# Copying gathered rows through ScalarE and gathering into half-chunk buffers in a two-layer relational graph network

## The chip, the core and the metric

The kernel runs on one core of a Trainium2 chip. The metric is device time in microseconds (us), from the start of the program on that core to its end. Five engines work in parallel, each through its own instructions in order: TensorE (PE in the profile; PEld is its weight load, which overlaps the matmuls), VectorE (DVE), ScalarE (ACT), GpSimd (POOL) and SyncE (SP). They are kept in step by semaphores: an instruction can wait until others have raised a semaphore, and raises one itself when it is done. POOL issues the gathers, SP the regular transfers.

## The reference

The kernel computes a relational graph network of two layers over 50,000 nodes with 128 features, followed by a residual layer norm. There are 16 relations whose matrices are mixtures of 8 bases, and 800,000 random edges and 50,000 self loops, sorted by their target.

```python
def _rgcn_layer(h, src, dst, rel, basis, w_comp, loop_w, bias):
    W = jnp.einsum('rb,bio->rio', w_comp, basis)
    seg = dst.astype(jnp.int32) * N_REL + rel.astype(jnp.int32)
    agg = jax.ops.segment_sum(h[src], seg, num_segments=N_ENT * N_REL)
    agg = agg.reshape(N_ENT, N_REL, -1)
    msg = jnp.einsum('nri,rio->no', agg, W)
    out = msg + h @ loop_w + bias
    return jax.nn.relu(out)
h = layer(layer(x))                       # two layers with their own weights
return _layernorm(x + h, axis=-1)
```

## The kernel before

The kernel does not sum by relation. For each of the 8 bases it sums, for every node, the rows of its neighbours weighted by the basis's share in the edge's relation, and then multiplies the 8 sums by the 8 basis matrices. The self loops are treated apart ("own", line 794), so that 800,000 edges are gathered in each of the two layers.

The unit of work is a tile of 128 edges. Ten tiles (K) make a chunk, and a layer has 625 chunks (C), so both layers together have 12,500 tiles. The edges are in the order of their targets. A chunk's first and last five tiles form two halves. For each chunk:

- POOL issues ten gathers (`gather`, line 260): each is an indirect DMA that fetches 128 rows of 512 bytes by a list of indices into one [128, 128] slice of a buffer `rows[...]`. There are four such buffers of ten tiles (GATHERS = 4). At chunk c, the ten gathers of chunk c+2 are issued (FETCH = 2, lines 1090 to 1093), into the buffer that chunk c-2 used. The first of them goes to the slice that PE reads last, so it carries the wait for PE's last matmul of chunk c-2. Each gather also waits until the gather eight earlier has landed, since there are eight semaphores ("lanes") for them.
- DVE builds the weighted one-hot matrices of a chunk (`hot_of`, lines 988 and 995: 128x2400 numbers, three buffers), two chunks ahead.
- PE multiplies, tile by tile, the gathered rows (as the loaded weights) by the tile's one-hot matrix (128x240): line 1112. The products of each half accumulate in a PSUM bank `pa` (six banks in layer 1, four in layer 2). In the trace each such matmul has two records.
- DVE adds the products to the running sums `ring` (`add`, line 1016, four adds of 128x240 for a chunk). They are queued eight tiles after the chunk's last matmul (ADDED = 8).

Around this runs the work of groups of 512 nodes, 98 in each layer: ScalarE lays out the group's own features (line 787) and DVE multiplies them into the ring (line 794) with a table that SP loads (line 776, 1 MB each); once a group's edges are all added, ScalarE copies its 128x4096 sums out of the ring (`copy`, line 814); PE multiplies them by the bases (line 818) on top of the loop weights (line 828); ScalarE applies relu (line 833); PE turns the result back (line 845), and it is stored (lines 853 to 863; in layer 2 with the layer norm, lines 611 to 622). ScalarE also widens the gather indices once for 16 chunks (`indexed`, line 951; a cast at line 953) and, in layer 1, moves the weights of the edges (line 694).

The order on PE, POOL, DVE and ScalarE is written out by hand (line 982). The loop over chunks emits the gathers and matmuls; everything else is put into a heap of events by `later(time, ...)` with times counted in tiles (ten for a chunk), and `go_on` emits what is due after each tile. So each engine's queue holds the events between the tiles at fixed places, in order.

Of the kernel before, what the change touches and what calls it, by code (L numbers as in the profile page):

```python
# [40 lines left out]
F32 = mybir.dt.float32  # L41
# [10 lines left out]
P = 128  # L52
# [4 lines left out]
K = 10  # L57
# [6 lines left out]
FETCH = 2  # L64
AT = 8
PER = 5
# [1 line left out]
BANK = 512  # L68
WEIGHTS = AT * PER * 8
BITS_AT_ONCE = 168  # L70
GATHERS = 4
J = 4
AHEAD = 16
EACH = 2 * len(WINDOWS)
# [20 lines left out]
def tile_rgcn_resnorm(  # L95
# [15 lines left out]
    nc = tc.nc  # L111
    N, D = x.shape
# [3 lines left out]
    C = -(-M // (K * P))  # L116
# [31 lines left out]
    consts = ctx.enter_context(tc.tile_pool(name="consts", bufs=1))  # L148
# [110 lines left out]
    def gather(to, of, idx):  # L259
        return nc.gpsimd.indirect_dma_start(  # L260
            out=to, out_offset=None, in_=of, in_offset=bass.IndirectOffsetOnAxis(ap=idx, axis=0)
        )
# [11 lines left out]
        return bass.AP(tensor=edges.tensor, offset=edges.offset + j * E + first, ap=ap)  # L274


    rows = [consts.tile([P, K, D], F32, name=f"g{i}") for i in range(GATHERS)]
    src = consts.tile([P, 2 * C * HALF], U16, name="src")
    key = consts.tile([P, 2 * C * HALF], U8, name="key")

# [312 lines left out]
    def count_up(pool):  # L593
        pick = pool.tile([P, 2], F32, name="pick")
        nc.vector.tensor_reduce(pick[:, 0:1], squares, AX.X, OP.add)
        nc.vector.tensor_reduce(pick[:, 1:2], picked, AX.X, OP.add)
        total = banks.take()
        nc.tensor.matmul(total[:1, :2], ones[:, 0:1], pick, start=True, stop=True)
        off = pool.tile([1, 2], F32, name="off2")
        nc.vector.tensor_scalar(off[:, 0:1], total[:1, 0:1], float(N), None, op0=OP.not_equal)  # L600
        nc.vector.tensor_scalar(
            off[:, 1:2], total[:1, 1:2], float(E + 2 * NG * (P + 1) + 2 * C), None, op0=OP.not_equal
        )
        nc.vector.tensor_tensor(bad, off[:, 0:1], off[:, 1:2], op=OP.max)
# [19 lines left out]
    def chunked():  # L624
        with (
# [5 lines left out]
            def ks(c):  # L631
                return min(K, -(-M // P) - c * K)
# [7 lines left out]
            def behind_of(c):  # L640
                return ADDED if c < C - 2 else PER
# [285 lines left out]
            def done(steps):  # L927
                for _ in steps:
                    pass
# [18 lines left out]
            index = {}  # L948

            def indexed(n, b, copy):  # L950
                first_of, end_of = b * AHEAD * K, min(C, (b + 1) * AHEAD) * K
                index[n, b] = hp.tile([P, AHEAD * K], I32, name="index", bufs=3)
                return copy(index[n, b][:, : end_of - first_of], src[:, first_of:end_of])
# [28 lines left out]
            ordered.enter_context(tc.manual_schedule(engines={mybir.EngineType.PE, mybir.EngineType.Pool, mybir.EngineType.DVE, mybir.EngineType.Activation}))  # L982
            for n, of in enumerate((x, H1)):

                def hot_of(c):
                    pm = batches[c // BATCH].pm
                    own = fixed[:, WN : WN + K * WN].rearrange("e (k w) -> e k w", w=WN)
                    nc.vector.tensor_tensor(  # L988
                        own,
                        grid[:, None, :].to_broadcast([P, K, WN]),  # L990
                        key[:, c * K : (c + 1) * K, None].to_broadcast([P, K, WN]),
                        op=OP.is_equal,
                    )
                    hot = hp.tile([P, K, NB, WN], F32, name="hot", bufs=3)
                    nc.vector.tensor_tensor(  # L995
                        hot,
                        pm[:, c % BATCH * K * NB : (c % BATCH + 1) * K * NB].rearrange("e (k b) -> e k b", b=NB)[:, :, :, None].to_broadcast([P, K, NB, WN]),
                        own[:, :, None, :].to_broadcast([P, K, NB, WN]),
                        op=OP.mult,
                    )  # L1000
                    hots[c] = hot
# [23 lines left out]
                def added_up_to(now):  # L1025
                    while behind and behind[0][0] <= now:
                        for one in sorted(behind.pop(0)[1], key=lambda one: (-one[1], one[2])):
                            add(*one)
# [20 lines left out]
                def go_on(now):  # L1049
                    while events and events[0][0] <= now:  # L1050
                        _, _, what, args = heapq.heappop(events)
                        what(*args)
# [10 lines left out]
                for c in range(C):  # L1063
                    if c >= 2:
                        later(K * (c - 2) + ADDED, hot_of, c)
# [14 lines left out]
                for c in range(C):  # L1080
                    if (c + FETCH + 3) % AHEAD == 0 and c + FETCH + 3 < C:
                        indexed(n, (c + FETCH + 3) // AHEAD, nc.scalar.copy)
                    if n == 0 and c == C - AHEAD // 2:
                        indexed(1, 0, nc.scalar.copy)
                    if n == 0 and c:

                        next(coming, None)
                        while ready[0] + 1 < len(ROWS) and 2 * min(C, c + FETCH + AHEAD + 4) > ROWS[ready[0] + 1]:
                            next(coming)
                    for to in range(0 if c == 0 else c + FETCH, min(C, c + FETCH + 1)):  # L1090
                        buffer = (n * C + to) % GATHERS
                        for k in (PER, *range(PER), *range(PER + 1, K)) if to + 1 < C else range(K):
                            gather(rows[buffer][:, k, :], of, index[n, to // AHEAD][:, to % AHEAD * K + k : to % AHEAD * K + k + 1])
                    g = rows[(n * C + c) % GATHERS]
                    if c == 0:
                        hot_of(0)
                        hot_of(1)
                    hot = hots.pop(c)
                    mine_of = []
                    for half in range(2):  # L1100
                        pa = banks.take(Once(added, c), OWN[n])
                        tiles = [(i, j) for i, (j0, j1) in enumerate(PARTS_OF) for j in range(j0, j1)]
                        tiles = [(i, j) for i, j in tiles if half * PER + j < ks(c)]
                        if c + 1 < C:
                            tiles.reverse()
                        mine = [[t for t in tiles if t[0] == i] for i in range(len(PARTS_OF))]
                        for at in range(PER):
                            if at < len(tiles):
                                i, j = tiles[at]
                                j0, j1 = PARTS_OF[i]  # L1110
                                w, before = WINDOWS[i], NB * sum(WINDOWS[:i])
                                nc.tensor.matmul(  # L1112
                                    pa[:, before : before + NB * w],
                                    g[:, half * PER + j, :],
                                    hot[:, half * PER + j].rearrange("e b w -> e (b w)"),
                                    start=(i, j) == mine[i][0],
                                    stop=(i, j) == mine[i][-1],
                                )
                            now = c * K + half * PER + at
                            if at == PER - 1:  # L1120
                                mine_of.extend((c, half, i, pa) for i in range(len(PARTS_OF)) if mine[i])
                                if half:
                                    behind.append((now + behind_of(c), mine_of))
                            added_up_to(now)
                            if n == 0 and c == 0:
                                for _ in range(2 if now < K - 1 else P):
                                    if next(first_runs, started) is started:
                                        started.clear()
                                        break
                            if c or now == K - 1:  # L1130
                                go_on(now)
                    if n == 0 and c == 3:
                        beginning.close()
                    if n == 0 and c == C - 1:
                        done(coming)
                        count_up(pr)
# [9 lines left out]
    def summed():  # L1146
        L1 = dram.tile([N, D], F32, name="L1")
        L2 = dram.tile([N, D], F32, name="L2")
        with tc.tile_pool(name="io", bufs=2) as io, tc.tile_pool(name="sbf", bufs=2) as sb:
# [152 lines left out]
            nodes(L2, norm, also=x)  # L1302

    chunked()
    wrong = nc.values_load(bad[0:1, 0:1], min_val=0, max_val=1)
    with tc.If(wrong > 0):
# [40 lines left out]
```

## Time and profile before

| | |
|---|---|
| time, median of 3 runs | 18022.98 us (18019.99 to 18026.41) |
| profiled execution | 17926.77 us, span 17925.0 us |
| mean granted TensorE clock | 0.718 |
| PE busy, matmuls | 9549.2 us (53%) |
| DVE busy | 7645.9 us (43%) |
| ACT busy | 1608.6 us (9%) |
| POOL busy | 11865.7 us (66%) |
| gathers | 12500, of which 6250 in each layer |
| bytes moved | 1525.45 MB, mean 85 GB/s |

The busy times are of one execution. No engine is busy more than two thirds of the time, so the time is set by how the engines wait for each other. Such waits are read from the groups of instructions, where each group has its busy time, the mean duration of one instruction in ns, and then the idle time of its engine just before the instructions with what ended it; and from the list of waits, which has the total in us, how often, and the longest. "issue" there is idle time in which the profile shows nothing that the engine waited for, and "remote" a wait that ended by a signal that the profile could not put down to an instruction.

### The profile page before, as it was taken

What the parts mean: (1) busy time and instruction counts of PE and PEld (TensorE: products, weight loads), DVE (VectorE), ACT (ScalarE), POOL (GpSimd) and SP (SyncE); (2) the same over time, 40 slices, a digit from 0 to 9 for tenths busy, and PEclk for the clock granted to TensorE, in tenths of its full rate; (3) what the DMA queues carried; (4) which work ended last, traced back from release to release, by engine and by line L of the source; (5) the groups of instructions that cost most, each with busy time, mean ns of one, the idle gap of its engine ahead of it and who ended that gap; (6) DMA issues with size and microseconds to landing.
All of it is one profiled execution on the core that took longest, in us unless ns stands there. A gap on an engine that the chain in (4) does not pass through costs nothing.

```text
span 17925.0 us, 102973 instructions
## 1 busy us (share of the span) xinstructions
PE 9549.2 (53%) x31567; PEld 6859.0 (38%) x31567; DVE 7645.9 (43%) x11001; ACT 1608.6 (9%) x2031; POOL 11865.7 (66%) x12540
## 2 busy tenths in 40 slices
PE   4555555555555555555545555555555555555555
PEld 3443334333333434343333333333333333333333
DVE  5554445454333433343334443444444344444433
ACT  1011101001000100000000000000000000000000
POOL 6666666666666666666666666666666666666666
PEclk7777777777777777777777777767777777777777
DMA  3333333333222222222222222222222222222222
GB/s 106 93 96 96 95 95 92 92 92 89 85 85 85 87 85 85 83 85 86 81 80 82 82 81 81 82 81 82 80 80 79 82 82 82 82 82 82 82 80 70
DMA packets 790743, 1525.45 MB, mean 85 GB/s; under 512 B 227861, under 2 KB 294279, under 8 KB 790182
## 3 DMA queue, kind: packets, MB, share of 16 engines
q0 software_dynamic: 401872, 826.89, 16.4%
q1 hardware_dynamic: 386566, 691.28, 11.5%
q8 instruction: 255, 4.18, 0.1%
q14 instruction: 306, 2.51, 0.0%
q10 hardware_dynamic: 1744, 0.60, 0.0%
HBM read 1390.94 MB, written 126.92 MB: 85 GB/s over the span
## 4 chain that ended last, share of the span: by engine, by line
another core or an unknown queue 42%; DVE 20%; issue 18%; POOL 11%; PE 7%; DVEq 1%; DMA 1%; ACT 1%; POOLq 0%; SPq 0%; ACTq 0%
POOL g L260 11%; DVE ring L1016 7%; DVE hot L995 5%; PE pa L1112 5%; DVE ring L794 3%; DVE fixed L988 2%; PE pn L818 2%; DVE fixed L336 1%; DVE word L339 1%; DVEq L1010 1%; ACT own L814 0%; DVE st L611 0%; DVE mv L612 0%; DVE t L856 0%
## 5 line engine op out<-in xcount | busy, mean ns | idle before, releaser
L1112 PE MATMUL pa<-hot,g 128*128 128x240 f32 x25000 | 7472.3, 439 | 6872.5 <-DVE ring L1016 3493.8
L1112 PEld LDWEIGHTS pa<-hot,g 128*128 128x128 f32 x25000 | 5631.8, 231 | 9201.2 <-issue 4431.8
L260 POOL DMA_INDIRECT g<-in_x_dram,index x6250 | 5944.4, 951 | 2985.9 <-issue 1851.2
L260 POOL DMA_INDIRECT g<-H,index x6250 | 5896.6, 943 | 3004.5 <-issue 1884.4
L1016 DVE TENSOR_TENSOR ring<-pa,ring 128x240 f32 x5000 | 2035.0, 407 | 9874.9 <-remote 8341.1
L995 DVE TENSOR_TENSOR hot<-pm,fixed 128x2400 f32<-128x2400 f32 x1250 | 3317.6, 2654 | 58.1 <-remote 3.5
L818 PE MATMUL pn<-own,basis 128*128 128x512 f32 x3072 | 1823.4, 672 | 275.9 <-issue 272.4
L814 ACT COPY own<-ring 128x4096 f32<-128x4096 f32 x192 | 692.8, 3608 | 3102.3 <-DVE ring L1016 1937.3
L794 DVE TENSOR_TENSOR ring<-wide,pa 128x2048 f32<-128x2048 f32 (+1 forms) x386 | 876.4, 2271 | 64.4 <-DMA wide<-CW 36.8
L818 PEld LDWEIGHTS pn<-own,basis 128*128 128x128 f32 x3072 | 653.6, 215 | 416.0 <-issue 362.3
L682 PE MATMUL pa<-each,is_rel 128*128 128x128 f32 x1570 | 321.8, 353 | 637.1 <-DVE ring L1016 408.0
L988 DVE TENSOR_TENSOR fixed<-fixed,key 128x300 f32<-128x300 f32 x1250 | 584.1, 467 | 0.1
L682 PEld LDWEIGHTS pa<-each,is_rel 128*128 128x128 f32 x1570 | 289.7, 257 | 683.8 <-DVE ring L1016 431.9
L833 ACT ACTIVATE oT<-pn,bias_of 128x512 f32<-128x512 f32 x194 | 133.1, 686 | 3836.2 <-remote 2962.7
L787 ACT COPY pa<-hT 128x512 f32<-128x512 f32 x392 | 227.9, 589 | 2592.8 <-DVE ring L1016 1647.9
L845 PE MATMUL pa<-ident,oT 128*128 128x128 f32 (+1 forms) x784 | 157.7, 328 | 298.9 <-DVE ring L1016 167.8
L828 PE MATMUL pn<-hT,loop 128*128 128x512 f32 x392 | 246.7, 698 | 95.2 <-issue 92.8
L746 ACT COPY hT<-pa 128x512 f32<-128x512 f32 x98 | 105.2, 1073 | 1859.5 <-remote 1226.9
L614 ACT ACTIVATE sd<-mv,eps 128x4 f32<-128x4 f32 x98 | 29.1, 297 | 2565.8 <-DVE st L611 1413.5
L845 PEld LDWEIGHTS pa<-ident,oT 128*128 128x128 f32 (+1 forms) x784 | 127.5, 209 | 342.1 <-DVE ring L1016 182.4
L339 DVE COPY_PREDICATED word<-fixed,word 128x168 int32<-128x168 int32 (+3 forms) x540 | 182.3, 338 | 18.7
L622 ACT ACTIVATE t<-t,nm,rs 128x128 f32<-128x128 f32 x392 | 161.4, 482 | 283.7 <-DVE nm L619 118.2
(140 smaller groups left out, 1600.2 us busy)
## 6 DMA issues: line engine op xcount, KB each, us to landing
wide<-CW SPq DMA_DIRECT2D x388, 1024.0 KB
g<-in_x_dram,index POOLq DMA_INDIRECT x6250
g<-H,index POOLq DMA_INDIRECT x6250
rows<-in_x_dram SPq DMA_DIRECT2D x194, 256.0 KB
PM<-pm SPq DMA_DIRECT2D x157, 160.0 KB
pm<-PM SPq DMA_DIRECT2D x157, 160.0 KB
H1T<-oT SPq DMA_DIRECT2D x97, 256.0 KB
H<-t SPq DMA_DIRECT2D x97, 256.0 KB
```

The costliest lines, as they stand in the source:

```text
L260: return nc.gpsimd.indirect_dma_start(out=to, out_offset=None, in_=of, in_offset=bass.IndirectOffsetOnAxis(ap=idx, axis=0))
L339: moved = nc.vector.copy_predicated(word[:, a : a + k], bit[:, :k], word[:, a + step : a + step + k])
L682: nc.tensor.matmul(of[:, :, :, (j - j0) * NB : (j - j0 + 1) * NB], self.is_rel[:m, j * P : (j + 1) * P], each[:m], start=True, stop=True,)
L794: nc.vector.tensor_tensor(wide if self.late else into, wide, self.laid.pop(b)[:, None, :cnt].to_broadcast([P, AT_ONCE, cnt]), op=OP.mult,)
L814: nc.scalar.copy(self.sums, ring[:, :, at : at + cnt])
L818: nc.tensor.matmul(self.pn[:, a:e], BASIS[:, b, :], self.sums[:, b, a:e], start=False, stop=b == NB - 1)
L828: nc.tensor.matmul(self.pn[:, a:e], LOOP, self.hT[:, a:e], start=True, stop=False)
L845: nc.tensor.transpose(self.po[:m, j * D : (j + 1) * D], by_place[:, j, :], ident)
L988: nc.vector.tensor_tensor(own, grid[:, None, :].to_broadcast([P, K, WN]), key[:, c * K : (c + 1) * K, None].to_broadcast([P, K, WN]), op=O ...
L995: nc.vector.tensor_tensor(hot, pm[:, c % BATCH * K * NB : (c % BATCH + 1) * K * NB].rearrange("e (k b) -> e k b", b=NB)[:, :, :, None].to_ ...
L1016: nc.vector.tensor_tensor(into, pa[:, before : before + NB * w].rearrange("d (b w) -> d b w", w=w), into, op=OP.add,)
L1112: nc.tensor.matmul(pa[:, before : before + NB * w], g[:, half * PER + j, :], hot[:, half * PER + j].rearrange("e b w -> e (b w)"), start=( ...
```

## The change

Four buffers of ten tiles become five buffers of five tiles (GATHERS = 5), and a pool of three further buffers of five tiles ("mid") is added, so that the gathered rows take as much memory as before (40 tiles). `fetched(u)` issues the five gathers of half u, and `passed_on(u)` has ScalarE copy the five tiles of half u, one [128, 128] slice at a time, from the gather buffer to a mid buffer. TensorE's matmuls read the mid buffer. At each half u of the loop the gathers of half u+4 are issued first, then the copies of half u, then the matmuls of half u. The four halves before are fetched at the start of a layer.

The gather buffer of half u is used again by half u+5, as soon as ScalarE has copied half u out; the gathers' waits are for ScalarE (and their lane), no longer for TensorE. ScalarE's copies wait for their gather to have landed, and the first of five also for TensorE's matmuls of three halves before, which read the mid buffer last. TensorE's first matmul of a half waits for ScalarE's copies. DVE's instructions and their order are the same. In the changed file, line 995 is the copy, 1029 the add, and 1125 the matmul.

```diff
--- before.py
+++ after.py
@@ -68,7 +68,7 @@
 BANK = 512
 WEIGHTS = AT * PER * 8
 BITS_AT_ONCE = 168
-GATHERS = 4
+GATHERS = 5
 J = 4
 AHEAD = 16
 EACH = 2 * len(WINDOWS)
@@ -274,7 +274,7 @@
         return bass.AP(tensor=edges.tensor, offset=edges.offset + j * E + first, ap=ap)
 
 
-    rows = [consts.tile([P, K, D], F32, name=f"g{i}") for i in range(GATHERS)]
+    rows = [consts.tile([P, PER, D], F32, name=f"g{i}") for i in range(GATHERS)]
     src = consts.tile([P, 2 * C * HALF], U16, name="src")
     key = consts.tile([P, 2 * C * HALF], U8, name="key")
 
@@ -982,6 +982,19 @@
             ordered.enter_context(tc.manual_schedule(engines={mybir.EngineType.PE, mybir.EngineType.Pool, mybir.EngineType.DVE, mybir.EngineType.Activation}))
             for n, of in enumerate((x, H1)):
 
+                def fetched(u):
+                    if u >= 2 * C:
+                        return
+                    for k in (PER - 1, *range(PER - 1)):
+                        at = (u // 2 % AHEAD * 2 + u % 2) * PER + k
+                        gather(rows[(2 * n * C + u) % GATHERS][:, k, :], of, index[n, u // 2 // AHEAD][:, at : at + 1])
+
+                def passed_on(u):
+                    to = sb.tile([P, PER, D], F32, name="mid", bufs=3)
+                    for k in range(PER):
+                        nc.scalar.copy(to[:, k, :], rows[(2 * n * C + u) % GATHERS][:, k, :])
+                    return to
+
                 def hot_of(c):
                     pm = batches[c // BATCH].pm
                     own = fixed[:, WN : WN + K * WN].rearrange("e (k w) -> e k w", w=WN)
@@ -1087,17 +1100,17 @@
                         next(coming, None)
                         while ready[0] + 1 < len(ROWS) and 2 * min(C, c + FETCH + AHEAD + 4) > ROWS[ready[0] + 1]:
                             next(coming)
-                    for to in range(0 if c == 0 else c + FETCH, min(C, c + FETCH + 1)):
-                        buffer = (n * C + to) % GATHERS
-                        for k in (PER, *range(PER), *range(PER + 1, K)) if to + 1 < C else range(K):
-                            gather(rows[buffer][:, k, :], of, index[n, to // AHEAD][:, to % AHEAD * K + k : to % AHEAD * K + k + 1])
-                    g = rows[(n * C + c) % GATHERS]
+                    if c == 0:
+                        for u in range(GATHERS - 1):
+                            fetched(u)
                     if c == 0:
                         hot_of(0)
                         hot_of(1)
                     hot = hots.pop(c)
                     mine_of = []
                     for half in range(2):
+                        fetched(2 * c + half + GATHERS - 1)
+                        g = passed_on(2 * c + half)
                         pa = banks.take(Once(added, c), OWN[n])
                         tiles = [(i, j) for i, (j0, j1) in enumerate(PARTS_OF) for j in range(j0, j1)]
                         tiles = [(i, j) for i, j in tiles if half * PER + j < ks(c)]
@@ -1111,7 +1124,7 @@
                                 w, before = WINDOWS[i], NB * sum(WINDOWS[:i])
                                 nc.tensor.matmul(
                                     pa[:, before : before + NB * w],
-                                    g[:, half * PER + j, :],
+                                    g[:, j, :],
                                     hot[:, half * PER + j].rearrange("e b w -> e (b w)"),
                                     start=(i, j) == mine[i][0],
                                     stop=(i, j) == mine[i][-1],
```

## The prediction

> **What bounds the kernel now.** I read the page's first part (no engine busy over 66%), then the groups of instructions and the list of waits, then the timelines of POOL, DVE and PE. From the page, groups (busy us, mean ns | idle before):
>
> ```profile
> L1112 PE MATMUL pa<-hot,g 128*128 128x240 f32 x25000 | 7472.3, 439 | 6872.5 <-DVE ring L1016 3493.8
> L260 POOL DMA_INDIRECT g<-in_x_dram,index x6250 | 5944.4, 951 | 2985.9 <-issue 1851.2
> L260 POOL DMA_INDIRECT g<-H,index x6250 | 5896.6, 943 | 3004.5 <-issue 1884.4
> L1016 DVE TENSOR_TENSOR ring<-pa,ring 128x240 f32 x5000 | 2035.0, 407 | 9874.9 <-remote 8341.1
> ```
>
> and from the list of waits (us in all, times, longest):
>
> ```profile
> DVE ring L1016 <- remote: 8341.1, 558, 31.3
> POOL g L260 <- issue: 3735.6, 11552, 7.0
> POOL g L260 <- remote: 1835.4, 416, 9.1
> PE pa L1112 <- DVE ring L1016: 3493.8, 458, 29.9
> POOL g L260 <- PE pa L1112: 153.1, 35, 6.2
> POOL g L260 <- DMA H<-t: 35.6, 1, 35.6
> POOL g L260 <- DVE turns L522: 11.5, 1, 11.5
> ```
>
> The gathers occupy POOL's whole span: 11,841 us busy and 5,990 us idle before them. A piece of POOL's timeline (start, us, idle before) shows how that idle time is made up:
>
> ```profile
> 12054.47 0.94 POOL L260 DMA_INDIRECT g<-H,index  x1 [6.86 <-remote]
> 12055.72 0.94 POOL L260 DMA_INDIRECT g<-H,index  x1 [0.30 <-issue]
> ...
> 12090.67 0.94 POOL L260 DMA_INDIRECT g<-H,index  x1 [0.30 <-issue]
> 12096.95 0.94 POOL L260 DMA_INDIRECT g<-H,index  x1 [5.34 <-remote]
> ...
> 12139.47 0.94 POOL L260 DMA_INDIRECT g<-H,index  x1 [5.38 <-PE pn L818]
> 12181.22 0.94 POOL L260 DMA_INDIRECT g<-H,index  x1 [4.61 <-remote]
> ```
>
> From 12054.47 to 12090.67 lie 29 steps, 1.248 us each: 0.94 and a gap of 0.30. Then comes a pause of 5.34 us: 30 gathers take 42.5 us, 1.417 each. Over the whole span 12,500 gaps of 0.30 are 3,750 us; less the start (11.5) and the change of layer (35.6), 5,990 − 3,750 − 47 = 2,193 us are pauses. Their number: 416 ended by "remote", 35 by PE, and of the "issue" row 3,736 − 11,552 × 0.30 = 270 us, about 60 more: some 510, of 4.3 us each, one for 25 gathers. So the time is 12,500 × 1.249 = 15,613 us of streaming plus 510 pauses.
>
> A pause is POOL waiting at a chunk's first gather for PE to have finished the chunk four before. But PE is not slow there. The timelines of PE, DVE and POOL around one pause:
>
> ```profile
> 5978.56 1.79 PE L1112 MATMUL pa<-hot,g 128*128 128x240 f32 x8
> 6009.41 3.17 PE L1112 MATMUL pa<-hot,g 128*128 128x240 f32 x7 [29.07 <-DVE ring L1016]
> ```
>
> ```profile
> 5979.22 2.65 DVE L995 TENSOR_TENSOR hot<-pm,fixed 128x2400 f32<-128x2400 f32 x1
> 6007.61 1.74 DVE L1016 TENSOR_TENSOR ring<-pa,ring 128x240 f32 x4 [25.74 <-remote]
> ```
>
> ```profile
> 6001.52 0.94 POOL L260 DMA_INDIRECT g<-in_x_dram,index  x1 [0.30 <-issue]
> 6008.34 0.94 POOL L260 DMA_INDIRECT g<-in_x_dram,index  x1 [5.88 <-issue]
> ```
>
> PE's matmuls stop at 5980.35 and DVE is free at 5981.87, yet the adds of those products start at 6007.61, when POOL has been quiet for over five microseconds; PE then waits for the adds. What PE has finished becomes known to the others only when POOL pauses. I see this again and again (DVE's 558 waits for "remote", 8,341 us); DVE's signals arrive at once. What holds PE's signals the trace does not tell. The cycle is therefore: POOL streams until its buffers are full by what it has been told of PE, goes quiet, PE's signals come through together, DVE and PE catch up, POOL resumes 0.73 us after (6007.61 to 6008.34).
>
> **The change part by part.** Prices of ScalarE's work, from its groups:
>
> ```profile
> L814 ACT COPY own<-ring 128x4096 f32<-128x4096 f32 x192 | 692.8, 3608 | 3102.3 <-DVE ring L1016 1937.3 <-issue 629.2 <-DVE ring L808 433.1
> L787 ACT COPY pa<-hT 128x512 f32<-128x512 f32 x392 | 227.9, 589 | 2592.8 <-DVE ring L1016 1647.9 <-DMA hT<-H1T 556.8 <-issue 219.4
> L622 ACT ACTIVATE t<-t,nm,rs 128x128 f32<-128x128 f32 x392 | 161.4, 482 | 283.7 <-DVE nm L619 118.2 <-DVE rs L617 67.1 <-DVE hot L995 59.7
> PE 9549.2 (53%) x31567; PEld 6859.0 (38%) x31567; DVE 7645.9 (43%) x11001; ACT 1608.6 (9%) x2031; POOL 11865.7 (66%) x12540
> ```
>
> *The copies' price.* The two copies differ by 3,584 columns and 3.02 us: 0.842 ns a column. A copy of 128 columns is then 589 − 384 × 0.842 = 266 ns; the row of that very shape, with other operands, is 482. Five are 1.33 to 2.41 us; I take 1.33, the price from copies.
>
> *1. ScalarE as a load.* 12,500 copies are 3,325 us (to 6,025) on top of 1,609: 28 to 43% of the span.
>
> ```profile
> PE pa L1112 <- DMA g<-H,index: 108.1, 65, 13.9
> ```
>
> No bound by itself, and it costs nothing as long as PE has gathered tiles in store: its matmuls waited for gathers only 108 us in all of layer 2, since a pause only follows a full store. Without that cover, at each layer's start, it is one copy chain, 2 × 1.3 us.
>
> *2. The restart.* The gather that ends a pause no longer waits for PE, but for five copies, and these wait for the same late signal of PE, since the mid buffer three halves back must have been read. The chain per pause becomes PE's signal, five copies, POOL: 510 × 1.33 = 680 us, all on the path, since POOL, quiet, is what the end waits for. It could be 0 if the signals that come through in a burst let ScalarE run while POOL is let go by earlier copies; at 482 ns it is 510 × 2.41 = 1,229.
>
> The Trainium skill, "ScalarE: Activation LUTs", section "What ACT_TABLE_LOAD costs", gives an ACTIVATE with immediates 186 ns + 0.833 ns an element and an overlap of 93 ns back to back; an estimate from it for five is 1.09 us, and this term would be 560 us. L787 and L814 agree with its slope (0.842). Its "Advanced Engine Details and Errata", section "The Read-Write Bubble", speaks against the form of the change: ScalarE's time between instructions is not pipelined, so use 512 or more elements. One copy of 640 columns would by the rows be 0.70 us.
>
> *3. How far each runs on held signals.* Buffers hold 40 tiles in both. At a chunk's start POOL could before be 30 to 40 tiles ahead of PE, now 35 to 40 at each half: a slightly longer stretch, −36 pauses of 4.3 + 1.33 = 5.6 us at best, −200 us. But PE, which before could go on for about two chunks on what it knew (20 tiles, by DVE's adds and the banks), now has at most three mid buffers, 15 tiles, past the last signal that ScalarE received. If that shortens a stretch from 25 to 20 gathers, there are 127 more pauses, +711 us. I take 25 more, +140, as the two work against each other.
>
> *4. What stands in ScalarE's queue.* The copies stand in one in-order queue behind `copy` (3.6 us), `relu`, `lay` and the norm's steps, each of which waits for PE or DVE. Of those, L814 is the long one; 192 times 3.6 us is 691 us at most, nothing if it falls into streaming. A pause takes 2,193 of 17,925 us, 12%, but the signals it waits for come through in pauses; I take a sixth, +115. Conversely these steps, 9% of ScalarE before, are now behind copies; PE's banks wait for them, at 1.33 us a time, within the pause counted.
>
> *5. The rest.* POOL issues the same 12,500 gathers with the same lanes; five at a time for ten, a wait at each half; the gap of 0.30 already holds a wait per gather. DVE's instructions stand as before, SP's transfers too; nothing moves past SP's queue. PE loses its wait per gather and gets one per half: nothing.
>
> The sum: 680 + 140 + 115 = 935 us on the profiled 17,927, 18,862. The runs' median, 18,023, stands 0.54% above the profiled execution, so 18,960. With all low ends it is 17,727 (17,820 in runs), with all high ones 20,560 (20,670).
>
> **The rivals.**
>
> *Gathers that no longer stall (faster).* If ScalarE's waits for PE do get their signals while POOL streams, or if signals are held just because POOL itself waits on PE, POOL never pauses. The first gather and the last of each layer, from the instructions of line 260 (shortest, median, longest in ns; first and last start):
>
> ```profile
> L260 POOL DMA_INDIRECT g<-in_x_dram,index x6250: 938/944/3073, 35.9 to 8981.8; - x196
> L260 POOL DMA_INDIRECT g<-H,index x6250: 938/944/1130, 9018.4 to 17882.9; - x196
> ```
>
> So 15,613 us of streaming, 36 before the first gather, 36 at the change of layer and 42 behind the last: 15.73 ms; half the pauses gone, 16.8. For it: DVE's signals to POOL and PE come at once, and ScalarE's may. Against: DVE too waits for PE alone, not POOL, and its waits are the worst. It decides where a copy's wait for the mid buffer ends within a microsecond of PE's matmul during streaming.
>
> *Finer halves, no tax (slightly faster).* Restarts after the first freed half rather than a chunk, the copies done within the burst. The longest stretch without an interruption I found is 60 gathers in 83.7 us:
>
> ```profile
> 9018.36 0.94 POOL L260 DMA_INDIRECT g<-H,index  x1 [35.64 <-DMA H<-t]
> 9102.08 0.94 POOL L260 DMA_INDIRECT g<-H,index  x1 [9.14 <-remote]
> ```
>
> 1.395 each, 17.44 ms and 114 us of ends: 17.55, in runs 17.65.
>
> *Nothing changes.* The restart is hidden in a pace that something else sets: 18.02.
>
> *ScalarE's queue sets the pace (much slower).* If a copy is stuck behind a relu or an own copy that waits for PE's signals later than the mid's, POOL gets a chunk at a time. Such a short cycle exists:
>
> ```profile
> 12492.67 0.94 POOL L260 DMA_INDIRECT g<-H,index  x1 [4.59 <-remote]
> 12507.59 0.94 POOL L260 DMA_INDIRECT g<-H,index  x1 [2.74 <-remote]
> ```
>
> Ten gathers in 14.92 us, with the copies 16.25: 1,250 × 16.25 = 20.3 ms, in runs 20.5. For it: L814's and L833's long waits for PE and DVE. Against: a group (6.4 chunks) has only some six such steps.
>
> **How the numbers follow.** The tax of about 0.9 ms (18.3 to 19.9 in runs): 0.52. Stalls gone or halved (15.8 to 17.4): 0.15. Finer halves (17.4 to 17.98): 0.12. Nothing within 0.2%, which is about what a measurement of this kernel can tell: 0.06. ScalarE's queue (19.9 and up): 0.15. So faster 0.27, same 0.06, slower 0.67. The range, 16,900 to 20,000, leaves out most of the first rival and most of the last; the likeliest case's own is 18,300 to 19,900.
>
> **What would show it.** Right: POOL's idle time rises by 0.9 ms with its pauses ended by ScalarE's copies; their mean goes from 4.3 to about 5.6 us; some 530 pauses; DVE's "remote" waits stay near 8 ms; copies of 0.2 to 0.3 us; before a pause's end stand five copies in a row. Wrong: POOL's idle time falls toward 3,750 us (signals no longer held); copies of 0.45 us or more; pauses of under three microseconds or over 700 of them.

## The result and the profile after

The changed kernel takes 18,768 us (median of four runs, 18,737 to 18,809), the kernel before beside it 18,025 us (18,020 to 18,038): slower by a factor of 1.0413, with a 95% interval of 1.0389 to 1.0436. The forecast was 18,960 us, with a chance of 0.67 for slower. By these runs, side by side, the change costs 744 us. The profiled execution of the changed kernel took 18,750 us, span 18,748, 823 us more than that of before. The profile of before is of a quicker execution, 17,927 us, about 100 us below the runs it is set beside here, so some 80 us of every difference between the two profiles are not the change's.

The first lines and the groups of instructions of the changed kernel (busy us, mean ns of one | idle time of its engine just before them, and what ended most of it):

```profile
span 18748.2 us, 118038 instructions
PE 9479.9 (51%) x31567; PEld 6935.5 (37%) x31567; DVE 7646.4 (41%) x11001; ACT 4180.2 (22%) x14531; POOL 11869.0 (63%) x12540
...
L1125 PE MATMUL pa<-hot,mid 128*128 128x240 f32 x25000 | 7352.3, 442 | 7968.5 <-ACT mid L995 3409.5
L260 POOL DMA_INDIRECT g<-in_x_dram,index x6250 | 5947.1, 952 | 3491.8 <-issue 1793.7
L260 POOL DMA_INDIRECT g<-H,index x6250 | 5897.2, 944 | 3316.7 <-issue 1814.6
L1029 DVE TENSOR_TENSOR ring<-pa,ring 128x240 f32 x5000 | 2036.3, 407 | 10711.3 <-remote 8720.1
L995 ACT COPY mid<-g 128x128 f32<-128x128 f32 x12500 | 2692.6, 295 | 10049.7 <-issue 8661.0
```

POOL's gathers are as busy as before, to 3 us. Their idle time went from 5,990 to 6,808 us, by 818: that is nearly all that lies between the two profiles. No engine is busier than 63%, and ScalarE, with 22%, is far from a bound. The list of waits of the changed kernel (us in all, times, longest) says what POOL now waits for:

```profile
DVE ring L1029 <- remote: 8720.1, 562, 33.5
POOL g L260 <- issue: 3608.3, 11676, 4.2
PE pa L1125 <- ACT mid L995: 3409.5, 453, 22.8
POOL g L260 <- ACT mid L995: 3061.8, 589, 14.3
```

Before, 1,835 us of POOL's waits ended by "remote" signals and 153 by TensorE; now 3,062 us end by ScalarE's copies. But TensorE's signals are as late as they were: VectorE's waits for them are 8,720 us, against 8,341. (The row says "remote" and names no sender; that it is TensorE is read from what the adds of line 1029 need, TensorE's products.) The gathers wait for ScalarE alone, and ScalarE waits for TensorE.

In the starts of the 12,500 gathers I counted as a pause each step at least 1 us longer than the usual 1.249 us. Before there are 525 such pauses with 4.18 us each beyond the usual step, together 2,195 us; after, 563 with 5.35 us, together 3,014. The change of layer, some 35 us, is counted as one in each; without it the means are 4.12 and 5.30. A pause of the changed kernel, in the timelines of POOL, PE and ScalarE (start, us, idle before):

```profile
9815.17 0.95 POOL L260 DMA_INDIRECT g<-H,index  x1 [0.30 <-issue]
9816.43 0.94 POOL L260 DMA_INDIRECT g<-H,index  x1 [0.30 <-issue]
9823.93 0.94 POOL L260 DMA_INDIRECT g<-H,index  x1 [6.56 <-ACT mid L995]
```

```profile
9805.46 4.14 PE L1125 MATMUL pa<-hot,mid 128*128 128x240 f32 x10 [1.10 <-issue]
9809.43 1.02 PE L828 MATMUL pn<-hT,loop 128*128 128x512 f32 x2
9824.40 1.14 PE L1125 MATMUL pa<-hot,mid 128*128 128x240 f32 x2 [13.95 <-ACT mid L995]
```

```profile
9804.31 1.09 ACT L995 COPY mid<-g 128x128 f32<-128x128 f32 x5 [0.67 <-ACT t L622]
9822.56 3.10 ACT L995 COPY mid<-g 128x128 f32<-128x128 f32 x15 [17.16 <-issue]
```

TensorE's last matmuls on mid buffers are done by 9809.6. ScalarE hears of it 13 us later. POOL, its buffers full, goes quiet at 9817.4; 5.2 us later the copies start, and three halves' copies run back to back, since all three mid buffers turn out to be free together. Five copies take 1.10 us, and 0.27 us after the fifth POOL resumes. It waits for the fifth, not the first, because `fetched` issues a half's last slice first and `passed_on` copies that slice last; the other order was not run. Over the 557 pauses at a half's first gather, the quiet time is on average 3.99 us until the first copy, 1.10 us for five copies and 0.55 us from the last copy to the gather (median 0.27). That is 5.6 us with the usual gap of 0.30.

In 427 of them ScalarE began nothing but copies before the fifth, and the quiet time is 5.07 us. In 130 something else of ScalarE's queue began in the pause ahead of the copies, and it is 7.49; in 117 of these the first copy starts directly behind that instruction. The longest are those in which a 128x4096 copy began (25 of them, 10.8 us on average). Here is one, in the timelines of POOL, ScalarE and DVE:

```profile
9232.80 0.94 POOL L260 DMA_INDIRECT g<-in_x_dram,index  x1 [0.30 <-issue]
9244.46 0.94 POOL L260 DMA_INDIRECT g<-in_x_dram,index  x1 [10.72 <-ACT mid L995]
```

```profile
9239.59 3.61 ACT L814 COPY own<-ring 128x4096 f32<-128x4096 f32 x1 [20.24 <-DVE ring L808]
9243.10 1.09 ACT L995 COPY mid<-g 128x128 f32<-128x128 f32 x5
```

```profile
9237.38 1.74 DVE L1029 TENSOR_TENSOR ring<-pa,ring 128x240 f32 x4 [17.66 <-remote]
9239.15 0.41 DVE L808 TENSOR_TENSOR ring<-ring 128x240 f32<-128x240 f32 x1
```

The copies stand in ScalarE's queue behind line 814, which waits for VectorE's adds, which wait for TensorE's late signal. TensorE's signal arrives at 9237.4; what was a restart within a microsecond now takes the adds, line 808, 3.6 us of copying out, and the five copies.

### The profile page after: what moved, and what is told of

It reads as the page before. It is cut to its first block, busy times and chain, and to the rows that moved or that the text cites. A ratio compares the mean times of both kernels' runs of the same rounds, so it can differ in the third digit from the quotient of the medians.

```text
span 18748.2 us, 118038 instructions
## 1 busy us (share of the span) xinstructions
PE 9479.9 (51%) x31567; PEld 6935.5 (37%) x31567; DVE 7646.4 (41%) x11001; ACT 4180.2 (22%) x14531; POOL 11869.0 (63%) x12540
## 5 line engine op out<-in xcount | busy, mean ns | idle before, releaser
L1125 PE MATMUL pa<-hot,mid 128*128 128x240 f32 x25000 | 7352.3, 442 | 7968.5 <-ACT mid L995 3409.5
L1125 PEld LDWEIGHTS pa<-hot,mid 128*128 128x128 f32 x25000 | 5669.0, 233 | 10109.8 <-issue 4702.3
L995 ACT COPY mid<-g 128x128 f32<-128x128 f32 x12500 | 2692.6, 295 | 10049.7 <-issue 8661.0
L818 PE MATMUL pn<-own,basis 128*128 128x512 f32 x3072 | 1899.2, 696 | 380.0 <-issue 375.9
```

The source lines that it names most:

```text
L818: nc.tensor.matmul(self.pn[:, a:e], BASIS[:, b, :], self.sums[:, b, a:e], start=False, stop=b == NB - 1)
L995: nc.scalar.copy(to[:, k, :], rows[(2 * n * C + u) % GATHERS][:, k, :])
L1125: nc.tensor.matmul(pa[:, before : before + NB * w], g[:, j, :], hot[:, half * PER + j].rearrange("e b w -> e (b w)"), start=(i, j) == mine ...
```

## The experiments

My theory was the forecast's: a pause of POOL ends with TensorE's late signal, and the change puts ScalarE's copies behind that signal. The rivals were that waiting by halves or the shorter supply of three mid buffers makes the loss (whatever the copies take), and that ScalarE costs because of all its other work.

One thing has to be told first. The runs fell on several chips, and the kernel before itself took 15.76 ms on one of them and 17.9 to 18.04 ms on two others. Each ratio below is against the kernel before on the same chip.

### On a chip where the kernel before takes 15.76 ms

Half buffers alone, without copies:

```diff
-GATHERS = 5
+GATHERS = 8
-                    for k in (PER - 1, *range(PER - 1)):
+                    for k in range(PER):
...
-                    to = sb.tile([P, PER, D], F32, name="mid", bufs=3)
-                    for k in range(PER):
-                        nc.scalar.copy(to[:, k, :], rows[(2 * n * C + u) % GATHERS][:, k, :])
-                    return to
+                    return rows[(2 * n * C + u) % GATHERS]
```

> Of the change only the half buffers: eight gather buffers of five tiles (again 40 tiles), no mid buffers and no copies; TensorE reads the gather buffers, and the gathers wait for TensorE half by half. Theory (the copies are the tax: they stretch each pause from 4.2 to 5.4 us): pauses are back at about 4.2 us, and with 35 to 40 tiles of lead there are no more of them than the 525 of before: 17.8 to 18.1 ms. Rival (waiting by halves makes more and longer pauses): 18.5 ms or more without a single copy.

One copy for a half:

```diff
-                    for k in range(PER):
-                        nc.scalar.copy(to[:, k, :], rows[(2 * n * C + u) % GATHERS][:, k, :])
+                    nc.scalar.copy(to, rows[(2 * n * C + u) % GATHERS])
```

> The changed kernel with one copy of 128x640 for a half in place of five of 128x128. Theory: the chain that ends a pause is shorter. By the rows of before a copy of 640 columns is 0.70 us against 1.33 for five, 0.63 us less for each of 564 pauses: 0.35 ms less, 18.4 ms. Rival (the price is the extra engine in the chain or the three mid buffers, whatever the copies take): 18.7 to 18.8 ms. Second rival (ScalarE's queue is blocked most of the time by its other work): no change either, and the pauses end at other operations than the copy.

Ten copies for a half:

```diff
-                        nc.scalar.copy(to[:, k, :], rows[(2 * n * C + u) % GATHERS][:, k, :])
+                        for e in range(0, D, D // 2):
+                            nc.scalar.copy(to[:, k, e : e + D // 2], rows[...][:, k, e : e + D // 2])
```

> The changed kernel with ten copies of 128x64 for a half in place of five of 128x128. Theory: with 0.842 ns a column a copy of 64 columns is 0.295 - 0.054 = 0.24 us, ten are 2.4 us against 1.5: 0.9 us more for each of 564 pauses, 0.5 ms, 19.3 ms. Rivals: no change, 18.7 to 18.8 ms.

A memset behind each gather:

```diff
+    spacer = consts.tile([P, 1], F32, name="spacer")
...
         nc.gpsimd.indirect_dma_start(...)
+        nc.gpsimd.memset(spacer, 0.0)
```

> The changed kernel with one small memset (128x1) on POOL behind each gather, which spaces the gathers by 0.1 us or more (small POOL instructions took 0.14 to 0.24 us in the trace of before). Theory (TensorE's signals are held because POOL streams its gathers faster than something behind it drains, and come through when it lags): with 1.40 us a gather, about the long-run pace of before, few signals are held, the pauses go, and so does the copies' tax: 12,500 x 1.40 + 0.1 = 17.6 ms, 17.5 to 18.2. Rival (signals are held whenever POOL has gathers to issue, at any pace): the pauses stay and the spacing comes on top, 0.1 to 0.25 us x 12,500: 20.0 to 21.9 ms.

The changed kernel unaltered:

> The changed kernel once more, unaltered, beside the kernel before. In the runs before this one the kernel before took 15.76 ms, not 18.02, and POOL streamed without pauses. Theory (the change costs only through the chain that ends a pause, and a pause needs TensorE's signals to be held): where the kernel before takes 15.76 ms the change costs nothing, within 0.2%; where it takes about 18.0 ms, the ratio is again 1.04. Rival (the copies cost whatever the signals do): over 1% slower in both settings.

| kernel | us | ratio to before (95%) |
|---|---|---|
| before | 15,760 | |
| half buffers alone | 15,771 | 1.0007 (0.9997 to 1.0017) |
| one copy of 640 | 15,768 | 1.0005 (0.9996 to 1.0015) |
| ten copies of 64 | 15,763 | 1.0002 (0.9992 to 1.0011) |
| changed, memset behind each gather | 15,858 | 1.0062 (1.0046 to 1.0079) |
| changed kernel | 15,758 | 0.9997 (0.9988 to 1.0007) |

The numbers expected of the first four were all missed, since none of them had foreseen this setting; what was expected of the changed kernel, unaltered, came true. What they show instead is where the change has a price: on this chip, where no signal is held, it costs nothing, with one, five or ten copies a half. The changed kernel's page and list of waits there:

```profile
span 15760.3 us, 118038 instructions
L260 POOL DMA_INDIRECT g<-in_x_dram,index x6250 | 5945.4, 951 | 1914.5 <-issue 1795.1
L260 POOL DMA_INDIRECT g<-H,index x6250 | 5898.0, 944 | 1922.8 <-issue 1816.9
L995 ACT COPY mid<-g 128x128 f32<-128x128 f32 x12500 | 3360.9, 296 | 10547.5 <-DMA g<-H,index 5354.5
L1029 DVE TENSOR_TENSOR ring<-pa,ring 128x240 f32 x5000 | 2037.3, 407 | 7428.0 <-PE pa L1125 5616.4
```

```profile
POOL g L260 <- issue: 3612.0, 11857, 0.3
POOL g L260 <- ACT mid L995: 87.4, 287, 0.3
```

The gathers' idle time is 3,837 us, which is 12,500 gaps of 0.30 and 87 us more, the start and the change of layer among them; no wait for a copy is longer than 0.3. VectorE no longer waits for anything "remote", but for TensorE's own matmuls, and these wait for gathered tiles. POOL streams from end to end; 26 pauses are left. This bears out the first half of the theory (no held signal, no pause, no tax) and refutes the rival by which the copies cost whatever the signals do. The memset of 0.12 us sank into the gap of 0.30: the step grew by only 0.008 us, so this run tells nothing of a slower POOL.

### Held on purpose

To have long pauses wherever the run would fall, I made TensorE wait, in every third chunk, for the last tile that POOL can gather ahead. Kernel before:

```diff
-FETCH = 2
+FETCH = 3
...
                                 i, j = tiles[at]
+                                if half and at == 2 and c % 3 == 0 and c + 3 < C:
+                                    nc.tensor.matmul(pa[:, 480:510], rows[(n * C + c + 3) % GATHERS][:, K - 1, :], hot[:, 0, 0, :], start=True, stop=True)
```

> The kernel before with its gathers emitted one chunk earlier (FETCH = 3, the same waits) and, in every third chunk, a small extra matmul of TensorE ahead of the chunk's last three tiles, which reads the last tile gathered for the chunk three later; its product is not used. So TensorE cannot finish that chunk until POOL has filled all its buffers and gone quiet: a held signal made on purpose, 416 times. Theory: each costs POOL a pause of landing (2.0 us), extra matmul and three tiles (some 2.3 us), about 4.3 us: 15.76 + 416 x 4.3 = 17.5 ms. Rival (POOL's pauses are filled elsewhere): 15.8 ms.

The changed kernel (and in the same way the other two, from the kernels above):

```diff
                                 i, j = tiles[at]
+                                if half and at == 2 and c % 3 == 0 and 2 * c + 8 < 2 * C:
+                                    nc.tensor.matmul(pa[:, 480:510], rows[(2 * n * C + 2 * c + 8) % GATHERS][:, PER - 2, :], hot[:, 0, 0, :], start=True, stop=True)
...
-                        fetched(2 * c + half + GATHERS - 1)
-                        g = passed_on(2 * c + half)
+                        if 2 * c + half + 2 < 2 * C:
+                            mids.append(passed_on(2 * c + half + 2))
+                        fetched(2 * c + half + 2 + GATHERS)
+                        g = mids.pop(0)
```

> The changed kernel held in the same way (the extra matmul in each third chunk's second half reads the last tile gathered for the half seven later; copies and gathers are emitted two halves earlier, which lets POOL fill all its buffers). Theory: every pause is longer by five copies in a row, 5 x 0.295 = 1.5 us: 416 x 1.5 = 0.6 ms above the held kernel before, 18.1 ms. Rival (the copies are not on the way from TensorE's signal to POOL, since some other copy frees a buffer first): the held kernel before's time within 0.1 ms.

> The kernel with eight half buffers and no copies, held in the same way (half seven later). Theory: pauses as in the held kernel before, 17.5 ms within 0.15. Rival (half buffers by themselves lengthen pauses): the time of the held changed kernel, 18.1 ms.

> The held changed kernel with one copy of 128x640 for a half. Theory: one copy of about 0.70 us in the chain in place of 1.5 us: 416 x 0.70 = 0.3 ms above the held kernel before, 17.8 ms. Rival (a further engine in the chain costs, not what its copies take): the same as with five copies, 18.1 ms.

These fell on a chip where the kernel before took 17,924 us, so that the made holds came on top of the chip's own, and the expected totals, reckoned from 15.76 ms, do not apply; the differences are what can be compared.

| held kernel | us | ratio to before, not held (95%) | pauses, mean us, sum |
|---|---|---|---|
| before | 18,676 | 1.0419 (1.0389 to 1.0449) | 636, 4.56, 2,901 |
| half buffers alone | 19,404 | 1.0825 (1.0794 to 1.0856) | 880, 4.14, 3,646 |
| one copy of 640 | 19,915 | 1.1110 (1.1077 to 1.1142) | 842, 4.94, 4,162 |
| changed, five copies | 20,303 | 1.1326 (1.1293 to 1.1359) | 871, 5.23, 4,554 |

The gathers of the last (the changed kernel, held) and of the half buffers alone (held), by the page:

```profile
L260 POOL DMA_INDIRECT g<-in_x_dram,index x6250 | 5948.7, 952 | 4206.4 <-ACT mid L995 2377.8
L260 POOL DMA_INDIRECT g<-H,index x6250 | 5896.4, 943 | 4155.0 <-ACT mid L995 2148.4
```

```profile
L260 POOL DMA_INDIRECT g<-in_x_dram,index x6250 | 5958.3, 953 | 3751.0 <-issue 1820.8
L260 POOL DMA_INDIRECT g<-H,index x6250 | 5911.6, 946 | 3691.2 <-issue 1801.3
```

With the same half buffers and as many pauses, five copies make each longer by 1.09 us, which is what five copies take (1.10), and the kernel slower by 0.9 ms. One copy makes it 0.80 us longer. So copies are on the way from TensorE's signal to POOL, and in the held kernels their length counts; the rivals by which the pause does not depend on them fall. The sizes were missed: five copies were expected 0.6 ms above the held kernel before and came 1.6 above, one copy 0.3 and came 1.2. But half buffers alone were not at the held kernel before's time either: 0.73 ms above, with 244 more and shorter pauses. In this made setting the first rival was right too, for a loss of its own.

### On a chip where the kernel before takes 18.04 ms

The half buffers alone and the one copy were run again, unaltered, and the kernel before with a wider memset (128x128 for 128x1) behind each gather.

> The half buffers alone (eight gather buffers of five tiles, no copies, TensorE reads them) once more, for a setting in which the kernel before takes about 18.0 ms; where it takes 15.76, this is again 15.77 and tells nothing new. In the held kernels, half buffers alone gave 881 pauses of 4.14 us against 637 of 4.56, and the copies made 5.21 of the 4.14. Theory A (the copies are nearly all of the loss): about 1.07 us less than the changed kernel for each of 564 pauses, 0.6 ms: 18.15 ms, within 1% of the kernel before. Theory B (the finer granularity is a good part, as in the held kernels): 18.3 to 18.6 ms. Theory C (finer waits help without copies): under 17.95 ms.

> The changed kernel with one copy of 128x640 for a half, where the kernel before takes about 18.0 ms (elsewhere 15.77 ms again). From the held kernels (pauses of 4.93 us with one copy, 5.21 with five): 0.28 us less for each of 564 pauses, 0.16 ms below the changed kernel, 18.6 ms. From the copies' own durations (0.70 us against 1.48): 0.4 ms below, 18.3 ms. Rival (number and length of copies are of no account): 18.77 ms.

> The kernel before with a memset of 128x128 on POOL behind each gather. A memset of 128x1 took 0.11 us and fitted into the gap of 0.30 us between gathers; 128 columns are put at 0.25 us, so that a gather comes each 1.39 us (1.3 to 1.5). Theory (TensorE's signals are held because POOL issues gathers without a rest): the signals come through, VectorE's waits for a signal that the profile calls remote fall from 8 ms to under 2, the pauses go, and the time is 12,500 x 1.39 + 0.12 = 17.5 ms (16.4 to 18.9 by the pace it turns out to have). Rival (signals are held at any pace of POOL): the pauses of 2.2 ms stay on top: 19.7 ms or more.

| kernel | us | ratio to before (95%) | pauses, mean us, sum |
|---|---|---|---|
| before | 18,043 | | (525, 4.18, 2,195 in its profile, 17,927 us) |
| half buffers alone | 18,039 | 0.9998 (0.9988 to 1.0007) | 584, 3.93, 2,296 |
| one copy of 640 | 18,634 | 1.0321 (1.0304 to 1.0338) | 536, 5.36, 2,873 |
| changed, five copies (first measurement, before at 18,025) | 18,768 | 1.0413 (1.0389 to 1.0436) | 563, 5.35, 3,014 |
| before, memset of 128 columns | 18,121 | 1.0044 (1.0027 to 1.0061) | 412, 2.81, 1,160 |

The gathers and the copies of the half buffers alone, and of the one copy, by their pages:

```profile
span 18034.0 us, 104216 instructions
L260 POOL DMA_INDIRECT g<-in_x_dram,index x6250 | 5946.4, 951 | 3048.2 <-issue 1797.4
L260 POOL DMA_INDIRECT g<-H,index x6250 | 5896.6, 943 | 3048.2 <-issue 1838.1
```

```profile
span 18648.6 us, 113038 instructions
L260 POOL DMA_INDIRECT g<-in_x_dram,index x6250 | 5959.6, 954 | 3424.5 <-issue 1807.7
L260 POOL DMA_INDIRECT g<-H,index x6250 | 5914.1, 946 | 3252.2 <-issue 1822.9
L994 ACT COPY mid<-g 128x640 f32<-128x640 f32 x2500 | 1767.8, 724 | 10581.7 <-remote 5374.1
```

Half buffers alone cost nothing: by the runs side by side they take as long as the kernel before. Their 59 more pauses, each 0.25 us shorter, come to 101 us more than in the profile of before, which is itself of an execution about 110 us quicker. So the loss is made by passing the tiles through ScalarE and the mid buffers (theory A; B, drawn from the held kernels, does not carry over, and C found no gain). With one copy in place of five, three quarters of the loss stay, though a copy of 640 columns takes 0.72 us against 1.10 for five: the ratio falls from 1.0413 to 1.0321. The total is what the held kernels' pauses had led to expect, 18.6 ms, but not for that reason. It falls by fewer pauses, 536 for 563, not shorter ones (5.36 and 5.35 on average). In pauses in which ScalarE began nothing else the quiet time was 4.97 us for 5.07, and 8.2 for 7.5 in the others. The traces show where the shorter copying went: with one copy ScalarE starts it 4.40 us into a pause on average, with five it starts the first after 3.99, so the 0.38 us saved are lost ahead of the copy. Why is not shown. That the copies' length counts for so little here, and in the held kernels for as much as the copies take, leaves the greater part to the detour itself: TensorE's signal has to reach ScalarE, past whatever its queue holds, before POOL can be told. That part is argued. No run tells ScalarE's queue from the supply of only three mid buffers, since the half buffers alone drop both.

The memset of 128 columns took 0.22 us and made the step from gather to gather 1.338 us. Both its theories were wrong: the pauses did not go, and they did not stay on top. The page of this kernel:

```profile
span 18101.9 us, 115474 instructions
L262 POOL DMA_INDIRECT g<-in_x_dram,index x6250 | 6001.8, 960 | 1607.1 <-issue 1027.4
L262 POOL DMA_INDIRECT g<-H,index x6250 | 5957.7, 953 | 1555.9 <-issue 1047.0
L1019 DVE TENSOR_TENSOR ring<-pa,ring 128x240 f32 x5000 | 2037.3, 407 | 9991.8 <-remote 8536.6
L265 POOL MEMSET spacer<- 128x128 f32 x12500 | 2786.0, 223 | 128.3 <-remote 96.6
```

12,500 steps became longer by 0.089 us, 1.11 ms in all, and the pauses shorter by 1.04 ms against the profile of before (2,195 to 1,160); by the runs side by side this kernel is 78 us slower. TensorE's signals stayed late (8,537 us). So most of the time that POOL spends otherwise is taken from the pauses: from the first gather's start to the last one's, a gather comes each 1.43 us before, 1.44 with half buffers and 1.44 with the memset. In the changed kernel it is 1.49.

## Why the prediction came out right, and what was mis-sized

The direction and the place were right, and the size was a quarter too big, 937 us by the runs against 744: POOL's idle time, in pauses ended by ScalarE's copies, with TensorE's signals as late as before. In the profile's terms the forecast was 18,862 us and the execution took 18,750. The 0.54% that the forecast added for the runs over the profiled execution was no such ratio: the changed kernel's runs stand 0.1% above its profile. The 17,927 us of the profile of before is within what this kernel takes on the chip of the held runs (17,919 to 17,934) and below its runs beside the changed kernel (18,020 to 18,038); that it was taken on another chip is likely and not shown. Step by step, in differences between the two profiles, whose pauses differ by 818 us:

- **ScalarE as a load.** No bound, as forecast: it was 22% busy, for 28 to 43%. A copy by itself is 295 ns (forecast 266). Five back to back take 1.10 us, less than five times that, and less than the 1.33 of the sum. By the Trainium skill, "ScalarE: Activation LUTs", section "What ACT_TABLE_LOAD costs", the estimate was 1.09 us for five, and the trace agrees (1.09 to 1.10); for one copy of 640 columns an estimate by its formula is 719 ns, measured 724.
- **The restart.** The mechanism is as forecast (signal, five copies, POOL), but by this reckoning its term, 680 us, was too big. A pause with copies alone has a quiet time of 5.07 us, against 4.12 + 0.30 = 4.42 before: 0.65 us more, times 557 is 360 us. The first copy starts 3.3 us into such a pause, over a microsecond sooner than POOL resumed before, so part of the copies lies in time that was a pause anyway. Why the signal comes to ScalarE sooner is not shown. Against the half buffers alone, and over all pauses, it is otherwise: there POOL was quiet for 4.2 us, and here the first copy starts after 4.0, five copies take 1.10, and 0.55 more pass until the gather. So how the loss is split between this term and the queue's depends on the kernel it is held against.
- **Number of pauses.** Forecast 25 more, at 140 us, for the shorter supply of mid buffers; counted 38 more, at 4.12 us each 157. That is no evidence for the reason: the half buffers alone, which have no mid buffers, paused 59 times more.
- **ScalarE's queue.** Forecast 115 us, from the 128x4096 copy alone. Measured: 130 pauses with other work of ScalarE in them, each 2.42 us longer than the others: 315 us. Only in 25 of them did a 128x4096 copy begin; the others hold short steps (lines 746, 787, 614 and a few more), which cost by what they wait for and not by how long they take. In its proportion this term was mis-sized the most, nearly threefold, and in the direction in which the fourth rival pointed.
- **The sum** of these three is 832 us, for 935 forecast and 818 between the profiles (744 by the runs). Two errors, of −320 and +200, largely cancelled, so that the total came as near as it did is in part luck.
- **The rivals.** "Gathers that no longer stall" was put at 15.73 ms in the profile, and 15.76 ms is what the kernel before and all the variants without a memset take on the chip without held signals. The price was right but not its cause: it is no effect of the change. "Finer halves, no tax" fell: half buffers alone neither gain nor lose. "Nothing changes" is true of half buffers alone. "ScalarE's queue sets the pace" was put at 20.5 ms in runs and did not come; its mechanism is part of the loss, by the 315 us above.

What the forecast did not see is that the bound which it took from the trace (signals held while POOL streams) is not a property of the program. Its forecast was made for, and met, a setting in which that is so; on the chip without held signals the change costs nothing.

## What to carry to other kernels

A buffer that is "freed by another engine" still waits for whatever that engine waits for: follow the chain to its end, and count what is added between the late signal and the engine that stands still, the other work in the new engine's in-order queue included. An engine that is 22% busy cost 4% here because its instructions stand behind a late signal; on the chip where that signal was not late, the same instructions cost nothing. Before tuning against a wait, see whether it is there on every chip.

## What the runs showed of the hardware

- The same program, the kernel before, took 15.76 ms on one chip and 17.92 and 18.04 on two others. The changed kernel's profile has, on the first, a mean granted TensorE clock of 0.789 against 0.715, no wait of VectorE for a "remote" signal against 8,720 us, and 26 pauses of POOL against 563. What holds TensorE's signals on the others was not found. Issuing the gathers a little slower does not free them: at 1.338 us a gather VectorE waited 8,537 us for them, at 1.249 it was 8,341.
- Where signals are held, POOL's long-run pace stays at 1.43 to 1.44 us a gather whether it streams at 1.249 with long pauses (4.18 us on average) or at 1.338 with shorter ones (2.81), as though something behind it took that long. That is a reading of three kernels and not shown by itself.
- ScalarE's copies of 64, 128 and 640 columns took 241, 295 and 724 ns. Back to back, copies of 128 columns came some 0.2 us apart (five in 1.10 us).
